# Graph attention and hypergraph layer in one kernel: block transposes moved ahead of the output's normalizations on VectorE, and a store moved behind loads on SyncE

## The chip, the cores and the metric

The kernel runs on one core of one Trainium2 chip. The metric is the time on the device in microseconds (us), as the median of several runs. The core has five engines that run beside each other: TensorE (PE; its weight loads are a row of their own, PEld), VectorE (DVE), ScalarE (ACT), GpSimd (POOL) and SyncE (SP), which here only issues transfers. They meet at semaphores.

## The reference

For 128 graphs of 128 nodes, with 512 features per node, in float32, there are two layers, and each adds to its input and is normalized. Cut to what matters, for one graph:

```
feats = x @ W[h]                                      # 8 heads of 64
e     = leaky_relu(e_self[:, None] + e_neigh[None, :]) + (-1e10 where no edge)
att   = softmax(e)                                    # 128 x 128 per head
y     = layernorm(x + relu(concat_h(att @ feats) + b))

H     = adj != 0
prop  = D^-1 H B^-1 H^T                               # 128 x 128 per graph
h     = layernorm(relu(prop @ (y @ W1^T) + b1))       # 1024 hidden
out   = layernorm(y + (prop @ (h @ W2^T) + b2) + y)
```

## The kernel before

The graphs are taken in 64 pairs. Each pair goes through five stages ("lags" 0 to 4), each one period of the schedule long, so five pairs are at work at once. Everything is unrolled, and the program is one list of steps in an order written out by hand: a step of pair p is entered with a lag and a time within the period, its place is (p + lag) * 38.6 + time, and the list is sorted by that number and emitted in this order. The times fix only the order. Each engine takes its own instructions in the order of the list, and the semaphores are put in by the framework from the data.

The large products with the weights are done on TensorE with Strassen-like schemes of seven products for a pair (`chain`): `pf` makes the features of the attention, `ph` the hidden layer and `py` the output layer, each with accumulators X, Y and W in banks of PSUM. Sums of inputs (`xS`, `zS`, `hS`) come from GpSimd, sums of products from VectorE (`f_sum`, `h_sum`, `y_sum`).

The steps that matter here:

- `exponential` (ScalarE, L609) leaves the softmax's numerators of a graph in `nb`. `attend` (TensorE, L665) needs them transposed per head, as the weights of its matmuls. The transpose goes by way of DRAM: `e_write` stores `nb` to `ed` (L613), `e_read` loads it back so that blocks change places (`eb`, L621, four transfers of 128 KB), and `e_transpose` transposes within the 32x32 blocks on VectorE (`eT`, L630). Each graph g of the pair has two of them, q = 0 and 1, for four heads each. `eT` has one buffer, `eb` two.
- `attend` for g = 0 stands in TensorE's order behind four products of the feature chain of the following pair (`pfX` in the profile), and is followed by two more (`pfX`, `pfW`). The features are summed by `f_sum` (VectorE, L499).
- Just ahead on VectorE stands `h_sum` for (1, 0), at 16.4 (L810), a sum of the hidden layer's products.
- `o_norm` (lag 4, time 17.0) normalizes the finished output of a pair, `o`, with two instructions on VectorE (L715), one per graph, by the mean and by `rso`, which GpSimd works out from the variance (`rstds`, L712). It ends with the store of `o` (L985, 512 KB), issued by SyncE. `o` has two buffers.
- `load_blocks` (time 19.0) issues four loads of `x` in blocks (`xb`, L121, 128 KB each, one buffer), which `x_transpose` (VectorE, L373) turns into `xT`; `load_edges` (20.5) issues four loads of `ab` (L129). `write_nodes` (17.0) writes a small table (`dd_d`, L362). SyncE issues all of them in the order of the list, and an issue that waits holds up those behind it.

In the list the places around the change are these, as times in the period: `h_sum` 16.4, `o_norm` with its store 17.0, `write_nodes` 17.0, `e_transpose` of graph 0 at 18.1 and 18.15, `f_sum` 18.2, `load_blocks` 19.0, `load_edges` 20.5, `attend` of graph 0 at 20.65 and 20.7, `f_sum` 21.4, `e_transpose` of graph 1 at 21.5 and 21.55, `spread_rows` 25.0, `attend` of graph 1 at 25.95 and 26.8.

The first pair is transposed on TensorE instead, and the last pair has its `attend` later, at 24.25.

Of the kernel before, what the change touches and what calls it, by code (L numbers as in the profile page):

```python
# [20 lines left out]
def kernel(  # L21
# [279 lines left out]
    LAST = PAIRS - 1  # L301
    steps = []

    def step(lag, time, since=0, until=PAIRS):

        def keep(fn):
            steps.append((lag, time, fn.__name__, range(since, until), fn, ()))
            return fn
        return keep

    def at(lag, time, fn, *args, since=0, until=PAIRS):
        steps.append((lag, time, fn.__name__, range(since, until), fn, args))
# [331 lines left out]
        )  # L644

    for (g, q), tm, (lag, tl), (lagx, tx), te, tt in (
        ((0, 0), 31.0, (1, 33.2), (1, 36.1), 4.05, 18.1), ((0, 1), 32.2, (1, 35.0), (1, 36.7), 4.6, 18.15),
        ((1, 0), 34.2, (2, 2.05), (2, 2.1), 7.8, 21.5), ((1, 1), 35.4, (2, 6.0), (2, 7.3), 7.9, 21.55),
    ):
        at(1, tm, masked, g, q)  # L650
        at(lag, tl, leaky, g, q)
        at(lagx, tx, largest, g, q)
        at(2, te, exponential, g, q)
        at(2, tt, e_transpose, g, q, since=1)
# [59 lines left out]
    def normalize(s, key, t, g):  # L714
        nc.vector.tensor_scalar(  # L715
            t, t, s["mv", key][:, g, 0:1], s["rs", key][:, g:g + 1], op0=ALU.subtract,
            op1=ALU.mult,
        )
# [145 lines left out]
    def weigh(s, i, to, start):  # L864
# [3 lines left out]
          QU, 1, until=LAST)  # L868
# [112 lines left out]
    @step(4, 17.0, until=LAST)  # L981
    def o_norm(p, s):
        for g in range(2):
            normalize(s, "o", s["o"][:, g, :], g)
        nc.sync.dma_start(out[2 * p:2 * p + 2].rearrange("g n f -> n g f"), s["o"])  # L985


# [225 lines left out]
```

## Time and profile before

| | before |
|---|---|
| median of 3 runs | 2531.06 us (2530.25 to 2531.11) |
| profiled span | 2529.7 us |
| mean granted TensorE clock | 0.997 |
| transfers | 345.06 MB, 136 GB/s |
| `eT` transposes on VectorE | 252, mean 679 ns |
| normalizations of `o` on VectorE | 126, mean 1204 ns |
| `xT` transposes on VectorE | 124, mean 1106 ns |
| `pav` matmuls on TensorE | 2048, mean 274 ns |

A page of the profile tells of one execution. Its first part gives each engine's busy time and share of the span; the fourth part follows the chain of work that ended last back to the start and gives the shares of it by engine. Other views are asked of the trace: the list of waits (engine and line, what it waited for, total in us, how often, the longest), the timeline of an engine (start in us, duration, line, operation, output and inputs by the program's names, shapes, count, and in brackets idle time before it and what ended that), and the issues of SyncE, marked SPq, in the same form. Timeline rows that follow each other with the same line are merged, so the duration of a row with x16 is that of sixteen instructions together. Matmul ends are modelled; starts are recorded.

### The profile page before, as it was taken

Reading aid. Unit: us, or ns where it says so; the run is one execution under the profiler, and the core shown is the slowest. Engines: PE = TensorE matmul, PEld = TensorE weight load, DVE = VectorE, ACT = ScalarE, POOL = GpSimd, SP = SyncE. Lnnn points to the kernel's source line nnn. Section 1 sums busy time; section 2 is a strip of 40 time slices with the busy share of each in tenths; the row PEclk is TensorE's granted clock in tenths of the full one; section 3 lists DMA queues with packets and bytes.
Section 4 is the critical chain, followed back from the end, with each engine's and each line's share of the span. In section 5 each row is a group of like instructions: output and inputs, shape, how many; then the busy total and the mean of one; then the engine's idle time right before and its main releaser. Section 6 shows DMA issues by size and latency. Waiting matters only on the chain.

```text
span 2529.7 us, 48862 instructions
## 1 busy us (share of the span) xinstructions
PE 2500.1 (99%) x16225; PEld 2251.9 (89%) x16225; DVE 2032.7 (80%) x4580; ACT 1530.5 (60%) x4481; POOL 1818.4 (72%) x2060
## 2 busy tenths in 40 slices
PE   7999999999999999999999999999999999999998
PEld 5898998998998989989989999899899898998997
DVE  7978778878888887788788888887877878888765
ACT  4565665655756656657556566565575665665653
POOL 5767777777677777777776777777777777777774
PEclk9999999999999999999999999999999999999999
DMA  6444445445444444444454444444544444444431
GB/s 182 134 139 139 139 134 148 132 133 145 135 135 141 138 140 140 129 144 136 131 149 130 143 138 140 142 137 130 148 131 136 143 137 139 140 134 144 135 116 51
DMA packets 432748, 345.06 MB, mean 136 GB/s; under 512 B 153176, under 2 KB 382064, under 8 KB 432496
## 3 DMA queue, kind: packets, MB, share of 16 engines
q1 hardware_dynamic: 429024, 337.46, 45.1%
q10 hardware_dynamic: 3472, 4.47, 0.6%
q8 instruction: 130, 2.13, 0.4%
q14 instruction: 122, 1.00, 0.1%
HBM read 239.08 MB, written 102.73 MB: 135 GB/s over the span
## 4 chain that ended last, share of the span: by engine, by line
PE 96%; DMA 2%; POOL 1%; DVE 1%; issue 0%; ACT 0%; SPq 0%; ACTq 0%; POOLq 0%; DVEq 0%
PE phX L795 18%; PE pyX L476 17%; PE pav L665 9%; PE phW L795 9%; PE pfX L476 9%; PE pyW L476 9%; PE pz L760 5%; PE phY L795 4%; PE pfW L476 4%; PE pyY L476 4%; PE pq L961 4%; PE pfY L476 2%; PE pd L432 1%; DMA w<-in_w1t_dram 0%; PE py L1004 0%
## 5 line engine op out<-in xcount | busy, mean ns | idle before, releaser
L332 ACT COPY py<-pyX 128x257 f32<-128x257 f32 x189 | 70.8, 375 | 539.1 <-PE pyX L476 539.1
L795 PEld LDWEIGHTS phX<-zS,w_sb 128*128 128x128 f32 x3072 | 363.2, 192 | 32.3 <-issue 31.0
L795 PE MATMUL phX<-zS,w_sb 128*128 128x128 f32 x3072 | 374.4, 275 | 1.8 <-POOL xS L458 1.2
L848 POOL TENSOR_TENSOR sq<-sq 128x512 f32<-128x512 f32 (+2 forms) x384 | 343.7, 895 | 20.1
L609 ACT ACTIVATE nb<-nb,nm 128x128 f32<-128x128 f32 x1024 | 320.1, 391 | 16.1 <-DVE nm L601 16.1
L579 POOL TENSOR_TENSOR nb<-nb,neg 128x512 f32<-128x512 f32 x256 | 318.4, 1277 | 8.7 <-DMA nb<-rd 8.7
L595 ACT ACTIVATE nb<-nb,ft 128x128 f32<-128x128 f32 x1020 | 317.3, 389 | 8.1 <-POOL nb L579 8.1
L712 POOL TENSOR_TENSOR rso<-veo,mhalf 128x2 f32<-128x2 f32 x63 | 44.1, 700 | 371.6 <-DVE veo L710 371.6
L825 ACT ACTIVATE h<-h,vecs 128x128 f32<-128x128 f32 x768 | 244.9, 391 | 64.5 <-DVE h L810 64.5
L601 DVE TENSOR_REDUCE nm<-nb 128x4 f32<-128x512 f32 x256 | 174.6, 682 | 131.0 <-ACT nb L595 118.8
L665 PEld LDWEIGHTS pav<-ft,eT 128*128 128x128 f32 x2048 | 243.3, 191 | 29.8 <-PE pfX L476 24.1
L665 PE MATMUL pav<-ft,eT 128*128 128x65 f32 x2048 | 247.0, 274 | 2.2
L476 PE MATMUL pyX<-w_sb,hS 128*128 128x257 f32 x1008 | 242.5, 382 | 0.0
L476 PE MATMUL pyW<-w_sb,hS 128*128 128x256 f32 x1008 | 238.5, 378 | 1.5 <-DVE y L879 1.5
L476 PE MATMUL pyX<-w_sb,h 128*128 128x257 f32 x1008 | 239.5, 379 | 0.5 <-ACT py L332 0.5
L476 PEld LDWEIGHTS pyW<-w_sb,hS 128*128 128x128 f32 x1008 | 190.6, 189 | 29.2 <-POOL rsa L712 1.9
L689 POOL TENSOR_TENSOR y<-y,b_bc 128x512 f32<-128x512 f32 x128 | 162.2, 1268 | 65.7 <-DVE y L680 65.7
L476 PEld LDWEIGHTS pyX<-w_sb,h 128*128 128x128 f32 x1008 | 186.4, 190 | 25.5 <-ACT py L332 0.9
L476 PEld LDWEIGHTS pyX<-w_sb,hS 128*128 128x128 f32 x1008 | 186.1, 190 | 24.3
L373 DVE STREAM_TRANSPOSE xT<-xb 128x512 f32<-128x512 f32 x124 | 137.0, 1106 | 56.8 <-DMA xb<-in_x_dram 56.8
L783 POOL TENSOR_TENSOR zS<-zT 128x256 f32<-128x256 f32 x128 | 93.3, 729 | 112.6 <-ACT zT L772 112.6
L951 DVE SCALAR_TENSOR_TENSOR y<-y,rsh,bw_bc 128x512 f32<-128x512 f32 x126 | 148.7, 1218 | 31.3 <-POOL rsh L947 31.3
(174 smaller groups left out, 5836.0 us busy)
## 6 DMA issues: line engine op xcount, KB each, us to landing
nb<-rd SPq DMA_DIRECT2D x127, 512.0 KB
ed<-nb SPq DMA_DIRECT2D x126, 512.0 KB
eb<-ed SPq DMA_DIRECT2D x504, 128.0 KB
x<-in_x_dram SPq DMA_DIRECT2D x64, 512.0 KB
out_dram<-o SPq DMA_DIRECT2D x63, 512.0 KB
xb<-in_x_dram SPq DMA_DIRECT2D x248, 128.0 KB
a<-in_adj_dram SPq DMA_DIRECT2D x64, 128.0 KB
w<-in_adj_dram SPq DMA_DIRECT2D x128, 64.0 KB
```

Source lines behind the costliest of these rows:

```text
L373: nc.vector.transpose(s["xT"][:, g].rearrange("p k (b n) -> p k b n", b=NB), s["xb"][:, g * NB:(g + 1) * NB].rearrange("p b (f k) -> p k b ...
L476: nc.tensor.matmul(to[:, :n], lhs[:, k, :], rhs[:, k, :n], start=bool(start) and k == 0, stop=(k == nk - 1), skip_group_check=True,)
L579: nc.gpsimd.tensor_tensor(t, t, neg[:, :, None, :].to_broadcast([P, NB, HH, B]), op=ALU.add)
L595: nc.scalar.activation(t, t, AF.Prelu, bias=s["ft"][:, g, h, 0:1], alpha=SLOPE)
L601: nc.vector.tensor_reduce(s["nm"][:, g, hs], scores(p, s, g, hs).rearrange("p b h j -> p h b j"), AX.XY, ALU.max, negate=True,)
L609: nc.scalar.activation(t, t, AF.Exp, bias=s["nm"][:, g, h:h + 1])
L665: nc.tensor.matmul(t[:, h * (U + 1):(h + 1) * (U + 1)], s["eT"][:, g, q * HH + h, :], s["ft"][:, g, q * HH + h, 2:], start=True, stop=True,)
L689: nc.gpsimd.tensor_tensor(s["y"][:, g, :], s["y"][:, g, :], b0_bc, op=ALU.add)
L795: nc.tensor.matmul(to[:, m * N:(m + 1) * N], w[:, k, m * P:(m + 1) * P], rhs[:, k, :], start=bool(start) and m == 0 and k == 0, stop=(k == ...
L825: nc.scalar.activation(dst[:, k, :], src[:, k, :], AF.Relu, bias=b1_sb[:, c:c + 1])
L848: nc.gpsimd.tensor_tensor(t[:, :n, :], t[:, :n, :], t[:, n:2 * n, :], op=ALU.add)
L951: nc.vector.scalar_tensor_tensor(t, t, s["rs", "h"][:, g:g + 1], bw_bc.rearrange("p (j c) -> p j c", j=2), op0=ALU.mult, op1=ALU.add,)
```

## The change

The transposes of graph 0 move from 18.1 and 18.15 to 16.6 and 16.65, which is ahead of `o_norm` (17.0) and behind `h_sum` (16.4) in VectorE's order. The store of `o` leaves `o_norm` and becomes a step of its own at 19.5, behind `load_blocks` and ahead of `load_edges` in SyncE's order. No work is added or removed. It is meant to have `eT` ready earlier for `attend`, and to keep the loads of `x` from standing behind a store that waits for the normalizations.

```diff
     for (g, q), tm, (lag, tl), (lagx, tx), te, tt in (
-        ((0, 0), 31.0, (1, 33.2), (1, 36.1), 4.05, 18.1), ((0, 1), 32.2, (1, 35.0), (1, 36.7), 4.6, 18.15),
+        ((0, 0), 31.0, (1, 33.2), (1, 36.1), 4.05, 16.6), ((0, 1), 32.2, (1, 35.0), (1, 36.7), 4.6, 16.65),
         ((1, 0), 34.2, (2, 2.05), (2, 2.1), 7.8, 21.5), ((1, 1), 35.4, (2, 6.0), (2, 7.3), 7.9, 21.55),
     ):
...
     def o_norm(p, s):
         for g in range(2):
             normalize(s, "o", s["o"][:, g, :], g)
+
+    @step(4, 19.5, until=LAST)
+    def store(p, s):
         nc.sync.dma_start(out[2 * p:2 * p + 2].rearrange("g n f -> n g f"), s["o"])
```

## Prediction

> **What bounds the kernel now.** I read the page first, for the engine that carries the end.
>
> ```profile
> PE 2500.1 (99%) x16225; PEld 2251.9 (89%) x16225; DVE 2032.7 (80%) x4580; ACT 1530.5 (60%) x4481; POOL 1818.4 (72%) x2060
> ...
> PE 96%; DMA 2%; POOL 1%; DVE 1%; issue 0%; ACT 0%; SPq 0%; ACTq 0%; POOLq 0%; DVEq 0%
> ```
>
> TensorE is busy for 99% of the span and is 96% of the chain that ended last. So nothing that VectorE or SyncE does counts by itself; only what lets TensorE start a matmul sooner does. But matmul ends are modelled, so a late start can lie inside a row that looks busy. The second view is the list of waits, where I look for entries that recur once per pair.
>
> ```profile
> DVE xT L373 <- DMA xb<-in_x_dram: 56.8, 60, 2.1
> ...
> PEld pav L665 <- PE pfX L476: 24.1, 57, 0.4
> ...
> DVE o L715 <- POOL rso L712: 13.6, 60, 0.2
> ```
>
> The columns are total us, times, longest. Only the middle entry is TensorE's: the weight load of `pav` (the attention product, whose weights are `eT`) comes late in 57 pairs. The third view is TensorE's timeline around it, in the middle of the run and in the last pair that has the same order:
>
> ```profile
> 1199.63 1.05 PE L476 MATMUL pfX<-w_sb,xS 128*128 128x264 f32 x4
> 1200.72 1.97 PE L665 MATMUL pav<-ft,eT 128*128 128x65 f32 x16
> 1202.53 1.11 PE L476 MATMUL pfX<-w_sb,xT 128*128 128x264 f32 x4
> ```
>
> ```profile
> 2438.83 1.05 PE L476 MATMUL pfX<-w_sb,xS 128*128 128x264 f32 x4
> 2439.72 1.90 PE L665 MATMUL pav<-ft,eT 128*128 128x65 f32 x16
> 2441.45 1.11 PE L476 MATMUL pfX<-w_sb,xT 128*128 128x264 f32 x4
> ```
>
> From the start of one `pfX` row to the next it is 2.90 us in the first and 2.62 us in the second: 0.28 us are lost. The single matmuls show where. In the middle, the step from the last `pfX` matmul to the first `pav` is 419 ns and the next step 132 ns; undisturbed they are 222 and 57. So the late weight load costs 197 ns at once and 75 ns more at the next step, as the second load could not run ahead either.
>
> Who is late? The entry above names `pfX`, but that is only the last semaphore by time. TensorE's sequencer waits at L665 for a VectorE semaphore that came at 1200.585, 11 ns after the first transpose into `eT` ended (1200.574); the weight load starts at 1200.689. At 1239 the same distances recur. The fourth view, VectorE's timeline before that next `pav` (1239.44), shows why `eT` is late:
>
> ```profile
> 1235.41 0.68 DVE L810 TENSOR_TENSOR h<-ph,phW 128x512 f32<-128x512 f32 x1
> 1236.32 2.35 DVE L715 TENSOR_SCALAR o<-o,mvo,rso 128x512 f32<-128x512 f32 x2 [0.23 <-POOL rso L712]
> 1238.59 1.29 DVE L630 STREAM_TRANSPOSE eT<-eb 128x512 f32<-128x512 f32 x2
> ```
>
> The two normalizations of the output stand between `h_sum` and the transposes: 0.23 us of waiting for GpSimd and 2.35 us of work, on something no matmul reads. The fifth view is SyncE's issues:
>
> ```profile
> 1199.98 0.40 SPq L985 DMA_DIRECT2D out_dram<-o  x1
> ...
> 1200.94 2.34 SPq L121 DMA_DIRECT2D xb<-in_x_dram  x4
> 1203.32 1.93 SPq L129 DMA_DIRECT2D ab<-in_adj_dram  x4
> ...
> 1228.21 1.75 SPq L621 DMA_DIRECT2D eb<-ed  x4
> ...
> 1233.71 1.73 SPq L621 DMA_DIRECT2D eb<-ed  x4
> ...
> 1238.70 0.40 SPq L985 DMA_DIRECT2D out_dram<-o  x1
> ```
>
> The queue stands at the store from 1235.5 (end of the last `eb` issue) to 1238.70, until `o` is normalized, with the loads of `x` behind it.
>
> **What the Trainium skill says.** "TensorE: Matmul & The Clock Gate", section "Architectural detail": TensorE can pull weight loads ahead of running matmuls, while VectorE is strictly first in, first out. Both agree here: within a run a `pav` load starts some 55 ns ahead of its own matmul while the matmul before is still running, the undisturbed first one even 0.22 us ahead (2439.50 for 2439.72), and the transposes keep their place behind a waiting normalization. "Perfetto Trace Analysis", section "Tensor Engine Instruction": a matmul's end is computed from its size; hence I count starts only. "SBUF — State Buffer", section "Who interferes with whom": `tensor_scalar` in a two-port mode and GpSimd's operations exclude each other. The trace agrees for the normalization, 542 to 1494 ns for one shape, while the transposes stay at 658 to 711 ns. "DMA: Bandwidth & Descriptors", section "Queues, rings and completion order": on each DMA engine, one queue's descriptors are taken in ring order. The packets agree in order: `eb`, then the store, then `xb`.
>
> **The change part by part.**
>
> *Transposes of the first graph from 18.1 and 18.15 to 16.6 and 16.65.* Nothing is added; the order on VectorE becomes `h_sum` (16.4), two transposes, two normalizations (17.0), then the feature sums (18.2) as before. The transposes start at about 1236.1 in place of 1238.59, so they end 2.5 us earlier, the first at about 1236.8. The matmul needs it, undisturbed, at 1239.24. The margin is over 2 us, so the 197 and the 75 ns both go. Are the inputs there? The packets of `eb` for this graph end 5.5 to 7.1 us before the transposes start in the pairs I compared, and 3.3 us or more before `h_sum` ends in every pair. `eT` was last read by the second graph's `pav` (from 1206.26, 1.7 us long), 28 us before.
>
> How often: pairs 1 to 62 have this transition. Taking for each the time from its last `pfX` matmul to the first matmul after the 16 of `pav`, the two undisturbed ones (pairs 1 and 62) take 1954 ns, the other 60 between 2170 and 2242. The excess sums to 16.4 us, 274 ns per pair. All of it is on TensorE and so on the path.
>
> *Normalizations later.* They lose their 0.23 us wait (`rso` ends at 1236.28, the transposes at 1237.4) and end at about 1239.7 in place of 1238.67. Only the store waits for them. The feature sums behind start 0.23 us earlier, while TensorE moves forward 0.27 us: a net loss of slack of 0.04 us. The sum of `pfW` ends at 1201.82 and the next matmul that writes this bank loads its weights at 1203.25, so 1.4 us of slack hide that. Cost: nothing. How long the normalizations take beside GpSimd's new neighbours is unknown: between 2x542 and 2x1494 ns; I keep 2.35 us, and even 2.99 us stays inside the slack.
>
> *Store from 17.0 to 19.5.* It now stands behind four `xb` issues (2.3 us) and before the four `ab` issues. `xb` is issued from about 1236.0 in place of 1239.66; its buffer has been free since 1214.8. Behind the waiting store stand `ab`, then the row spread and the `nb` loads. The store can go at 1239.7, so `ab` goes at about 1240.1, in place of 1242.06: earlier too. VectorE's wait for `xb` (56.8 us over 60 times, 0.95 us each) should vanish. But after it no matmul in the pair waits for VectorE: `y` of this pair is read at 1218.73 and ScalarE has written it by 1216.5. So this part is worth nothing in time, and its new neighbour in the ring, `eb` of the second graph, is ahead of `xb`, its packets ending by 1237.2 while its transposes start at 1240.47.
>
> Sum: 16.4 us off. 2531.06 - 16.4 = 2514.7 us.
>
> **The rivals.**
>
> *Only the direct stall goes.* If the 75 ns are not a consequence of the late load but the matmuls' rhythm in this place, 60 x 0.197 = 11.9 us go: 2519.2 us. For it: a slow step can be made up by the following. Against: both undisturbed transitions show 222 and 57 with nothing made up later.
>
> *The gain is eaten by the next wait.* A load or a bank that was just in time now binds: about 2531 us, no change. For it: one wait hidden behind another is common. Against: the last pair shows a full distance without it, and the producers of `hS`, `zS`, `y` and `eb` that I looked at end 1.2 us or more before the matmul that first reads them.
>
> *Slower, because the late normalizations hold up the feature sums.* If these came so late that TensorE waited 0.5 us in each pair in place of 0.27, the time would be 2531.06 + 60 x 0.23 = 2545 us. That needs a slip of 1.9 us, or normalizations of 4.3 us together; the longest pair possible from the trace is 2.99.
>
> **How the numbers follow.** Full gain 0.83; direct stall only 0.10; eaten 0.03; slower 0.04. The lower end is the largest excess in every transition, 62 x 0.288 = 17.9 us, or 2513.2, less a little for the ends of the run: 2512.5. The upper end takes in the smaller gain with some more lost: 2520.5. Faster has the first two, 0.93; same 0.03; slower 0.04.
>
> **What would show it.** Right: the step into `pav` is 222 ns and the next 57 in all pairs; the wait of `pav` is gone from the list; the distance from pair to pair falls from 38.72 to about 38.45 us; the transposes start right after `h_sum`; VectorE's wait for `xb` is gone, without effect. Wrong: a new recurring wait of TensorE, a transpose waiting for `eb`, or `pav` late although `eT` is ready.

## The result, and the profile after

| | before | changed |
|---|---|---|
| median | 2531.09 us (2530.25 to 2531.29, 6 runs) | 2512.77 us (2512.5 to 2513.0, 6 runs) |
| ratio to before | | 0.9928, interval 0.9915 to 0.9941 |
| profiled span | 2529.7 us | 2510.2 us |
| VectorE's normalizations of `o`, mean of 126 | 1204 ns | 772 ns |

The changed kernel takes 18.3 us less; 16.4 were forecast. The page of the changed kernel (busy time by engine; shares of the chain that ended last):

```profile
PE 2484.8 (99%) x16225; PEld 2256.4 (90%) x16225; DVE 2019.9 (80%) x4580; ACT 1534.2 (61%) x4481; POOL 1824.3 (73%) x2060
...
PE 97%; DVE 1%; issue 0%; POOL 0%; ACT 0%; DMA 0%; POOLq 0%; DVEq 0%; ACTq 0%; SPq 0%
```

TensorE still carries the end, and its share is 99% as before: the lost time had been inside "busy" rows, so the share could not show it. Its timeline around `pav`, in a middle pair:

```profile
1227.37 1.05 PE L476 MATMUL pfX<-w_sb,xS 128*128 128x264 f32 x4
1228.26 1.90 PE L665 MATMUL pav<-ft,eT 128*128 128x65 f32 x16
1229.99 1.11 PE L476 MATMUL pfX<-w_sb,xT 128*128 128x264 f32 x4
```

From `pfX` to `pfX` it is now 2.62 us, where it was 2.90. Matmul by matmul, the step into `pav` is 222 or 223 ns and the next 56 or 57 in all 62 pairs that have this transition. From the last `pfX` matmul to the first after `pav` it is 1954 or 1955 ns in all 62 pairs, and from pair to pair 38.45 us where it was 38.72. (Ahead of this `pav` stand five products of the feature chain, not four, and two behind it; the argument needs only the last of the five.) VectorE's timeline before this `pav`:

```profile
1224.43 0.68 DVE L810 TENSOR_TENSOR h<-ph,phW 128x512 f32<-128x512 f32 x1
1225.03 1.30 DVE L630 STREAM_TRANSPOSE eT<-eb 128x512 f32<-128x512 f32 x2
1226.25 1.45 DVE L715 TENSOR_SCALAR o<-o,mvo,rso 128x512 f32<-128x512 f32 x2
1227.62 0.42 DVE L499 TENSOR_TENSOR ft<-pf,pfY 128x264 f32<-128x264 f32 x1
```

The transposes start right behind `h_sum` and end 1.9 us before `pav`. The two normalizations take 1.45 us in place of 2.35. And SyncE's issues:

```profile
1222.81 1.91 SPq L621 DMA_DIRECT2D eb<-ed  x4
1224.83 0.36 SPq L362 DMA_DIRECT2D dd_d<-dr  x1
1225.25 1.90 SPq L121 DMA_DIRECT2D xb<-in_x_dram  x4
1227.73 0.41 SPq L988 DMA_DIRECT2D out_dram<-o  x1
1228.18 2.40 SPq L129 DMA_DIRECT2D ab<-in_adj_dram  x4
```

The loads of `x` no longer stand behind the store. In the list of waits the entries of `pav` and of `xb` are gone, and VectorE has a new one:

```profile
DVE y L696 <- POOL y L689: 33.7, 63, 0.9
```

In place of `xb` it now waits in the same part of the pair, 0.53 us each time, for GpSimd's sum with the bias. The 57 us of waiting for `xb` were no part of the end: with the store alone moved, below, they go and the time stays.

Where the 18.3 us came from: 16.4 from the 60 late weight loads, and some 1.9 from pair 1, at the start. There the transposes also passed two instructions of `skip` (2.83 us beside GpSimd's squares), and two waits of TensorE near 78 and 93 us went from 0.43 to nothing and from 1.66 to 0.17 us. Other stalls of the first 70 us differ by up to 1 us between profiled runs either way, so from one pair of traces this part is only plausible; a run below tests it. The first part can be read directly: set side by side matmul by matmul, the changed kernel is 3.1 us ahead at 100 us and 19.5 us ahead at the end, so it gains 16.4 us from there on.

### The profile page after: what moved, and what is told of

Same layout as the page of the kernel before. It is cut to its first block, busy times and chain, and to the rows that moved or that the text cites. A ratio compares the mean times of both kernels' runs of the same rounds, so it can differ in the third digit from the quotient of the medians.

```text
span 2510.2 us, 48922 instructions
## 1 busy us (share of the span) xinstructions
PE 2484.8 (99%) x16225; PEld 2256.4 (90%) x16225; DVE 2019.9 (80%) x4580; ACT 1534.2 (61%) x4481; POOL 1824.3 (73%) x2060
## 4 chain that ended last, share of the span: by engine, by line
PE 97%; DVE 1%; issue 0%; POOL 0%; ACT 0%; DMA 0%; POOLq 0%; DVEq 0%; ACTq 0%; SPq 0%
PE phX L795 18%; PE pyX L476 17%; PE phW L795 9%; PE pfX L476 9%; PE pav L665 9%; PE pyW L476 9%; PE pz L760 5%; PE phY L795 4%; PE pq L961 4%; PE pfW L476 4%; PE pyY L476 4%; PE pfY L476 2%; PE pd L432 1%; PE pf L513 1%; PE py L1007 0%
## 5 line engine op out<-in xcount | busy, mean ns | idle before, releaser
L848 POOL TENSOR_TENSOR sq<-sq 128x512 f32<-128x512 f32 (+2 forms) x384 | 342.7, 893 | 20.1
L696 DVE SCALAR_TENSOR_TENSOR y<-y,x 128x512 f32<-128x512 f32 x128 | 153.7, 1201 | 35.0 <-POOL y L689 33.7
```

The costliest lines, as they stand in the source:

```text
L696: nc.vector.scalar_tensor_tensor(y, y, 0.0, s["x"][:, g, :], op0=ALU.max, op1=ALU.add)
L848: nc.gpsimd.tensor_tensor(t[:, :n, :], t[:, :n, :], t[:, n:2 * n, :], op=ALU.add)
```

## The experiments

The kernel before was run again beside each group. The columns of an added row are as in the fences above.

**The transposes alone.**

```diff
-        ((0, 0), 31.0, (1, 33.2), (1, 36.1), 4.05, 18.1), ((0, 1), 32.2, (1, 35.0), (1, 36.7), 4.6, 18.15),
+        ((0, 0), 31.0, (1, 33.2), (1, 36.1), 4.05, 16.6), ((0, 1), 32.2, (1, 35.0), (1, 36.7), 4.6, 16.65),
```

> The kernel before with the two transposes of graph 0 moved ahead of the normalizations, the store left where it was. Theory (the late transposes are all of it): 2512.8 us, within 0.5 us of the changed kernel; the step into pav is 222 ns and the next 57 in all pairs, while VectorE still waits for xb (some 50 us in total). Rival (the earlier loads of x give a part of the 18.3 us): about 2515 us or more.

Measured: 2513.27 us (2512.76 to 2514.89), ratio 0.9931 (0.9918 to 0.9943). `pav` steps 222 and 57; VectorE waits 74.5 us for `xb`, more than before. So the transposes give all of the gain that can be told apart from the spread of the runs.

**The store alone.**

```diff
+    @step(4, 19.5, until=LAST)
+    def store(p, s):
         nc.sync.dma_start(out[2 * p:2 * p + 2].rearrange("g n f -> n g f"), s["o"])
```

> The kernel before with the store alone moved behind the loads of x. Theory: 2531 us within 0.5, although VectorE's wait for xb (56.8 us) is gone; the step into pav stays 419 ns. Rival (the loads of x matter): 2529 us or less.

Measured: 2531.32 us, ratio 1.0 (0.9992 to 1.0008). The wait for `xb` is gone, and the step into `pav` is still 364 to 435 ns in 60 of the 62 pairs, all but the first and the last, as before: nothing gained.

**The transposes made later, in the order before.**

```diff
-    at(1, 18.2, f_sum, 0, 0, 0, "Y", since=2)
+    at(1, 18.05, f_sum, 0, 0, 0, "Y", since=2)
```

> The kernel before with one feature sum (L499, 0.39 us) put ahead of the transposes of graph 0, so that they end 0.31 to 0.39 us later still. Theory (pav waits for the first transpose alone): TensorE loses the same again in 60 pairs, 60 x 0.31 to 0.39 = 19 to 23 us, so 2550 to 2554 us. Rival (pav waits for its bank or for pfX, as the list of waits names it): 2531 us.

Measured: 2551.38 us (2551.06 to 2551.76), ratio 1.008 (1.0065 to 1.0096): 20.1 us more, inside what was expected. TensorE's timeline of this kernel:

```profile
1248.34 1.05 PE L476 MATMUL pfX<-w_sb,xS 128*128 128x264 f32 x4
1249.76 1.97 PE L665 MATMUL pav<-ft,eT 128*128 128x65 f32 x16 [0.37 <-DVE eT L630]
1251.57 1.11 PE L476 MATMUL pfX<-w_sb,xT 128*128 128x264 f32 x4
```

The gap is now long enough to show as idle time, and the view names VectorE's `eT`. So `eT` ends this wait, not `pfX`, as the list of waits of the kernel before had it. One feature sum ahead costs about what it moves the transposes, 0.33 us in each of 60 pairs.

**GpSimd's squares moved, the rest as before.** VectorE's order is untouched; only what runs beside the normalizations changes.

```diff
-            at(3, ((17.0, 17.1, 17.2), (26.0, 27.3, 28.0))[g][level], squares, g, level)
+            at(3, ((23.5, 23.55, 23.6), (26.0, 27.3, 28.0))[g][level], squares, g, level)
```

> The kernel before, VectorE's and SyncE's order unchanged, but GpSimd sums the squares of graph 0 (L848) behind the sums hS instead of during the normalizations. Theory (the normalizations are long, 2.35 us, because GpSimd's squares hold the port they share): the two take 1.0 to 1.3 us, the first transpose ends some 1.1 us earlier, 0.4 us before pav needs it, and most of the stall of 274 ns goes without any reordering on VectorE: about 2515 us. Rival (their length is their own, or another GpSimd instruction takes the squares' place): 2531 us, or slower if the later squares hold up what follows.

Measured: 2540.76 us (2539.28 to 2541.09), ratio 1.0038 (1.0024 to 1.0051): slower. VectorE's timeline and the list of waits say what happened:

```profile
1239.83 1.00 DVE L715 TENSOR_SCALAR o<-o,mvo,rso 128x512 f32<-128x512 f32 x2 [0.23 <-POOL rso L712]
1240.75 1.29 DVE L630 STREAM_TRANSPOSE eT<-eb 128x512 f32<-128x512 f32 x2
```

```profile
DVE y L696 <- POOL y L689: 100.1, 63, 2.7
...
PEld phX L795 <- ACT zT L772: 26.2, 62, 0.8
```

The first half of the theory held: the normalizations take 1.00 us together (mean of one 555 ns), and the step into `pav` is 222 with no change of VectorE's order. But the squares now stand before the sum with the bias on GpSimd, `y` comes late, and ScalarE's `zT` with it: the step of TensorE into `phX` is 0.39 us longer per pair (500 ns where it was 112). The time came out as the rival had it (later squares hold up what follows); the forecast of 2515 us was wrong because I had not asked what stands behind the moved squares.

**The squares behind the sum with the bias.**

```diff
-            at(3, ((17.0, 17.1, 17.2), (26.0, 27.3, 28.0))[g][level], squares, g, level)
+            at(3, ((24.2, 24.25, 24.3), (26.0, 27.3, 28.0))[g][level], squares, g, level)
```

> The kernel before with GpSimd's squares of graph 0 behind the sum with the bias (L689) of graph 0, so that the normalizations have the port to themselves but y isn't made late. Theory (the earlier try with the squares lost only because the bias, and with it y and zT, came 1.1 us late): pav steps of 222 and 57, no wait of phX for zT, about 2515 us. Rival (the squares moved cost somewhere else): 2531 us or more.

Measured: 2514.4 us (2512.89 to 2514.59), ratio 0.993 (0.9917 to 0.9944); normalizations 554 ns each, `pav` steps 222 and 57, no wait of `phX` for `zT`. So the same gain is to be had by shortening the normalizations as by passing them. The two were not run together; the changed kernel has no stall left in this place to remove.

**Only the first of the two transposes ahead.**

```diff
-        ((0, 0), 31.0, (1, 33.2), (1, 36.1), 4.05, 16.6), ((0, 1), 32.2, (1, 35.0), (1, 36.7), 4.6, 16.65),
+        ((0, 0), 31.0, (1, 33.2), (1, 36.1), 4.05, 16.6), ((0, 1), 32.2, (1, 35.0), (1, 36.7), 4.6, 18.15),
```

> The changed kernel with only the first transpose (heads 0 to 3) ahead of the normalizations, the second behind them. Theory (the stall is the first weight load's alone; the second four heads are needed 0.84 us after): pav undisturbed, 2512.8 us. Rival (the second half then comes late): some 0.2 to 0.7 us per pair, 2525 to 2555 us.

Measured: 2514.68 us (2513.79 to 2516.15), ratio 0.9933 (0.9919 to 0.9947). The `pav` stall is gone in all pairs: only the first weight load was late. In its trace the two early waits, at `pfW` and `pyW`, are there with 0.31 and 1.67 us, as the second transpose of pair 1 again stands behind `skip`.

**Pair 1 as before, in the changed kernel.**

```diff
+        ("e_transpose", 1, 0, 0): 133.9, ("e_transpose", 1, 0, 1): 133.95,
         ("nodes", 2): 141.0, ("write_nodes", 2): 143.0, ("nodes", 3): 150.0,
```

> The changed kernel with the transposes of graph 0 of pair 1 alone put back to their old place. Theory (what was gained beyond 16.4 us comes from pair 1's transposes, which no longer stand behind two instructions of skip beside GpSimd): the stalls of 0.43 us at pfW and 1.5 us at pyW near 78 and 93 us return, 2514.7 us. Rival (it comes from another place, or from chance at the start): 2512.8 us.

Measured: 2515.51 us (2514.83 to 2516.18), ratio 0.9935 (0.9922 to 0.9949). The stalls return at 78 us (0.43 us) and at 93 us (1.66 us). The other traces agree: both stalls are gone in the runs that have both transposes of pair 1 ahead of `skip` (the changed kernel, the transposes alone, the two runs with one normalization on each side, below), and both stand in the kernel before, here, and where only the first transpose is ahead. So the traces show the 1.9 us; the times point the same way, but the intervals of the two ratios overlap.

**One normalization on each side of the transposes, the store at its old place.**

```diff
+    at(4, 16.5, o_norm, 0, until=LAST)
+    at(4, 17.0, o_norm, 1, until=LAST)
...
+    @step(4, 17.0, until=LAST)
+    def store(p, s):
```

with the transposes at 16.6 and 16.65.

> The changed order, but with one of the two normalizations still ahead of the transposes of graph 0, and the store at its old place. Theory (the matmul needs the first transpose 2 us later than the changed kernel has it): the transposes end about 1.2 us later than in the changed kernel and still in time; pav steps of 222 and 57, about 2513 us. Rival (part of the stall returns): 2520 us or more.

Measured: 2536.07 us (2533.6 to 2540.09), ratio 1.0019 (1.0012 to 1.0026): slower. The time is in the range of the rival, but not for its reason: no part of the stall returned. `pav` is undisturbed in all 62 pairs, as the theory said, and yet all is lost elsewhere. The list of waits:

```profile
DVE xT L373 <- DMA xb<-in_x_dram: 147.2, 60, 3.0
...
PEld phX L795 <- ACT zT L772: 22.7, 46, 1.4
```

and the timelines of VectorE and ScalarE in one pair:

```profile
1234.69 1.48 DVE L715 TENSOR_SCALAR o<-o,mvo,rso 128x512 f32<-128x512 f32 x1 [0.23 <-POOL rso L712]
1236.09 1.29 DVE L630 STREAM_TRANSPOSE eT<-eb 128x512 f32<-128x512 f32 x2
1237.31 1.50 DVE L715 TENSOR_SCALAR o<-o,mvo,rso 128x512 f32<-128x512 f32 x1
```

```profile
1253.41 1.51 ACT L737 ACTIVATE y<-y,sh,rsa 128x512 f32<-128x512 f32 x2
1254.82 2.43 ACT L595 ACTIVATE nb<-nb,ft 128x128 f32<-128x128 f32 x8
1257.16 0.35 ACT L877 COPY y<-pyX 128x256 f32<-128x256 f32 x1
1257.41 1.07 ACT L772 COPY zT<-pz 128x512 f32<-128x512 f32 x2
```

Both normalizations now run into a long instruction of GpSimd (mean 1472 ns). The second ends at 1238.8, 0.8 us after this pair's `pav` has begun at 1237.97; in the kernel before it ended 0.8 us ahead of `pav`. The store waits for it, the loads of `x` wait behind the store, VectorE waits 2.5 us for `xb`, `y` is late, and on ScalarE `zT` stands in line behind `y`, eight steps of `nb` and a copy. TensorE waits at `phX`:

```profile
1258.04 2.05 PE L795 MATMUL phX<-zT,w_sb 128*128 128x128 f32 x16 [0.18 <-ACT zT L772]
```

The step into this `phX` is 459 ns where it is 112 undisturbed, 0.35 us lost. The loss is uneven, from nothing to 1.4 us in the pairs of this run; what makes it so is not shown.

**The same, with the store behind the loads of x.**

```diff
-    @step(4, 17.0, until=LAST)
+    @step(4, 19.5, until=LAST)
     def store(p, s):
```

> The kernel with one normalization on each side of the transposes, as in the run that came out slower, and with the store moved behind the loads of x as in the change. Theory (that run was slower only because the second normalization ended late, the store held the loads of x in SyncE's queue, and xT, y and zT came late in turn): VectorE's wait for xb is gone, no wait of phX for zT, pav steps of 222 and 57, about 2513 to 2515 us. Rival (the longer normalizations themselves push y late): 2530 us or more again.

Measured: 2513.49 us (2512.81 to 2513.99), ratio 0.993 (0.9913 to 0.9946). The wait for `xb` and that of `phX` for `zT` are both gone, while the normalizations are as long as in the run before (mean 1473 ns): their length alone costs nothing here. One issue moved in SyncE's queue is worth 22.6 us here and nothing in the order before.

## Why the prediction was right

*The bound and its cause.* Right. TensorE lost 274 ns in each of 60 pairs by a late weight load of `pav`, and the load waited for the first transpose. The run with the transposes later shows it with the opposite sign.

*The 75 ns of the second step.* Right: they went with the 197 in every pair, so the rival "only the direct stall" (2519.2 us) falls.

*The store is worth nothing.* Right for this change, by the runs of each part alone. My reason was too generous, though. I counted 2.2 us from the end of `y` to its first matmul, but the tight place is further along, in ScalarE's line. The kernel before:

```profile
1215.01 1.51 ACT L737 ACTIVATE y<-y,sh,rsa 128x512 f32<-128x512 f32 x2
1216.42 2.43 ACT L595 ACTIVATE nb<-nb,ft 128x128 f32<-128x128 f32 x8
1218.77 0.35 ACT L877 COPY y<-pyX 128x256 f32<-128x256 f32 x1
1219.82 0.59 ACT L772 COPY zT<-pz 128x512 f32<-128x512 f32 x1 [0.71 <-PE pz L760]
```

ScalarE idles 0.71 us before `zT`: that is about all that `y` may slip, and `zT` was not among the producers whose slack I had looked at. In the slower run `y` begins 2.50 us before its `pz` (1255.91) in place of 3.72 (1218.73), 1.2 us later; `zT` then begins 0.41 us later against `pz`, and TensorE loses 0.35 us of it at `phX`. So "the gain is eaten by the next wait" was nearer than the prediction had it; it takes normalizations that end late and a store left in front.

*The normalizations' length.* I kept 2.35 us; it is 1.45. The mechanism I cited (the Trainium skill, "SBUF — State Buffer", section "Who interferes with whom": whichever starts second waits for the whole instruction of the other) fits. In the kernel before, 124 of the 126 normalizations begin while a GpSimd instruction runs, and they end 279 to 286 ns after the end of that instruction, however early they began; in the changed kernel 125 do, and end 280 to 290 ns after. The two that meet none, before, take 542 and 543 ns. So about half of a normalization is left to do when GpSimd is done; why half and not all is not shown, and whether GpSimd waits in turn was not looked at. But I did not use it to see that, begun 1.0 us into the long square (1226.254 against 1225.273), the first would wait only for the rest of it.

*The sum.* The term that was too small is the number of places: I counted pair 1 as undisturbed because its `pav` was. Its transposes held up VectorE's later sums instead, and so two products. With these 1.9 us, 16.4 becomes 18.3. The measured 2512.77 us is 0.3 us above the lower end of my range, and it is in part luck that the range held it: that end stood for the largest excess in every transition, which no trace shows, and a gain in pair 1 was not in it.

## What to carry to other kernels

When an engine is 99% busy, look for a step between starts that differs from the same step in an undisturbed pair; here 274 ns hid in rows counted as busy, and the list of waits named the wrong releaser. Before moving a step, ask for each engine what stands in line behind it, and count slack at the tightest place down the line, not at the first reader. A change that is worth nothing alone can still be what keeps its neighbour's gain: test parts both alone and in orders where they are needed.

## What the runs showed of the hardware

- A normalization of 128x512 on VectorE takes 555 ns with GpSimd's squares elsewhere, 772 ns on average in the changed kernel, 1204 before and 1472 when both meet a long one: a factor of 2.7 by neighbours alone. One that begins beside a running GpSimd instruction ends 0.28 us after it (279 to 290 ns, 249 cases in the two kernels).
- A weight load that comes late costs TensorE at two matmuls. Undisturbed, the first load of `pav` starts 2 ns after the last `pfX` matmul has started (2439.501 against 2439.499); in the middle of the run before, it started 388 ns after (1200.689 against 1200.301). Of these 386 ns, TensorE lost 197 at the matmul itself and 75 at the following one.
